# Layer 1's neighbour sums in a two-layer graph kernel: from four parts in two PSUM banks to five parts in four

## The chip, the cores and the metric

The kernel runs on one core of a Trainium2 chip. The metric is the device time of the whole kernel in microseconds (us). Five engines of the core work side by side, each through its own program in order: TensorE (PE: matmuls, and weight loads, PEld), VectorE (DVE), ScalarE (ACT), GpSimd (POOL) and SyncE (SP). They meet through semaphores.

## The reference

`x` is 4096 x 64; `adj` is a 4096 x 4096 matrix of zeros and ones with about 8 ones in a row. Two layers run one after the other, each with a residual:

```python
h = relu(layernorm(x))                      # layer 0
w = adj / max(adj.sum(1), 1e-8)
log_ij = logmap(h[i], h[j])                 # on the Poincare ball, c = 1
x = x + expmap(0, einsum('ij,ijc->ic', w, log_ij) @ W0 + b0)

h = relu(layernorm(x))                      # layer 1
support = h @ W1
rank = cumsum(adj != 0, axis=1); deg = rank[:, -1:]
k = minimum(deg, 100); pos = rank - (deg - k)
w = mask * where(pos > 0, 0.5 ** (k - pos), 0)
x = x + w @ support + b1
```

Layer 0 needs a vector for each pair of neighbours; layer 1 is a product of a sparse 4096 x 4096 weight matrix with `support`. A neighbour's weight in layer 1 is a power of two set by its rank in the row.

## The kernel before, in words

All of it is one function, `tile_gnn_kernel`. Nodes are kept in 32 blocks of 128 rows, in four quarters of eight blocks (`QB = 8`). First `adj` is streamed in and turned into fp8 masks, `masks[q]`, one per quarter of rows (`load`: SP's DMA at L873, transposes at L888, ACT's copy at L891), and each row's neighbours are searched and listed (L917, L981 and others). A row's first six listed neighbours are its "ell" part; the further ones of long rows are the "tail", kept in extra columns for a quarter's blocks.

**Layer 0** then runs in units 0 to 16. A unit: `gather` (L1139) issues one indirect DMA on POOL for each list column (12 for the ell part of two blocks, 9 or 6 for tails in units 5 to 16), which fetches the neighbours' rows into the tile `g`, of which there are two; so the gathers of unit n start only when unit n-2 has done with its `g`, whose last reader is DVE's L1234 (and L1198 in some units). `tail_rows` makes one-hot tiles on ACT (L1156, L1163), transposes them on PE (L1169), copies them (L1170) and selects the tail's own rows with PE matmuls (L1178). `differ` subtracts on DVE (L1192, L1208, L1211) and squares on ACT (L1222). `weigh` starts with L1234, the sum of squares, and goes back and forth between DVE and ACT to L1251. `total` scales the tails' one-hots on ACT (L1261), sums tails on PE (L1266) and the ell part on DVE (L1281, L1288); `total_tail` is L1295.

**Between the layers**, `middle(m, stage)` takes a group of blocks, `groups = [(0,8),(8,8),(16,8),(24,6),(30,2)]`: stage 0 (L1314 and on) finishes layer 0's sum; stage 1 (L1334, transposes L1302, matmuls L1345) multiplies by W0 into a tile of the pool `ps_w` named `words`; stage 2 is tanh, residual and layernorm on DVE and ACT (L1353 to L1359, helpers up to L739); stage 3 multiplies by W1 (L1386, L1390 into `ps_t`) and splits the result into three bf16 terms by ACT (L1403) and DVE (L1405), which go to `sup[c]`. The rows are shifted by one, so the last block of each half of the matrix comes with its group, but the last of the other groups' eight only with the next group: group 0 alone fills seven blocks.

`step` (L1412) turns the masks of a quarter into the layer's weights by adding exponents on DVE, 15 of them a quarter.

**Layer 1's sums** are `collect(c, p, n)` (L1414): part `c` of the sum's terms, quarter `p` of the rows, pair `n` of its blocks. `sums` lists the parts as (first block, blocks, groups that must be ready): 16, 7, 6 and 3 blocks. For each of two row blocks, `nb` matmuls of 128 x 128 masks with 128 x 192 of `sup[c]` (L1422; in the last part one more with the bias, L1430) add up in a PSUM tile of 2 x 256 fp32 a partition, from the pool `ps_a` with two buffers. `pool` decides how it leaves: false, by DVE (L1441 sums the three terms, L1445 adds it to `acc`); true, by ACT (L1436 copies it to `mr` or `dg`) and three additions on POOL (L1438). Each part has 16 collects of 2 x `nb` matmuls: 1024 at L1422 altogether, 24 evictions by DVE and 40 by ACT and POOL. The first part is DVE's, the second and third ACT's and POOL's, the fourth half and half. After the last one a flag is read back and the kernel ends.

**The order.** `at(when, fn)` collects the whole work in a plan with a due time; collects are due 20 after the latest of their groups and quarter. The plan is sorted, gives each call a priority, and the tile framework's scheduler orders every engine's program by these and by what is ready in its own model of time. So an engine's order is fixed when the program is built; a late operand makes an engine wait at that instruction. In the built program of before, only 14 of the sums stand on PE ahead of unit 13's L1169; the other 498 of part 0 are spread from there on between the matmuls of the later units.

Of the kernel before, what the change touches and what calls it, by code (L numbers as in the profile page):

```python
# [11 lines left out]
F32 = mybir.dt.float32  # L12
# [7 lines left out]
P = 128  # L20
# [528 lines left out]
def kernel(  # L549
# [66 lines left out]
    with ExitStack() as fast:  # L616
# [174 lines left out]
        late = masks[NQ - 1].bitcast(F32).rearrange("p b c -> p (b c)")  # L791
# [44 lines left out]
        ps_a = fast.enter_context(tc.tile_pool(name="ps_a", bufs=2, space=PSUM))  # L836
        ps_w = fast.enter_context(tc.tile_pool(name="ps_w", bufs=2, space=PSUM))
# [7 lines left out]

        groups = [(0, 8), (8, 8), (16, 8), (24, 6), (30, 2)]

        sums = [(0, 16, (0, 1)), (16, 7, (2,)), (23, 6, (3,)), (29, 3, (4,))]


        def bf(at, n):
# [3 lines left out]
        sup, o = [], 0  # L855
        for c, (_, nb, _) in enumerate(sums):
            n = nb + (c == len(sums) - 1)
# [555 lines left out]

        def collect(c, p, n):  # L1414

            pool = 0 < c < len(sums) - 1 or (c == len(sums) - 1 and n >= 2)
            b0, nb, _ = sums[c]
            end = c == len(sums) - 1
            o = ps_a.tile([P, 2, 2 * P], F32, name="a_ps")
            for k in range(2):  # L1420
                for j in range(nb):
                    nc.tensor.matmul(  # L1422
                        o[:, k, 0:W3],
                        lhsT=masks[p][:, b0 + j, bass.ts(2 * n + k, P)],
                        rhs=sup[c][:, j, :],
                        start=(j == 0),
                        stop=(j == nb - 1 and not end),
                    )
                if end:
                    nc.tensor.matmul(  # L1430
                        o[:, k, 0:W3], lhsT=last, rhs=sup[c][:, nb, :], start=False, stop=True
                    )
            ab = acc[:, p * QB + 2 * n : p * QB + 2 * n + 2, :]
            if pool:
                ev = (lst if n % 2 else blk).tile([P, 2, W3], F32, name="dg" if n % 2 else "mr")
                nc.scalar.activation(ev, o[:, :, 0:W3], AF.Copy, scale=2.0**-W8_SHIFT)  # L1436
                for k in range(3):
                    nc.gpsimd.tensor_tensor(ab, ab, ev[:, :, k * D : k * D + D], ALU.add)  # L1438
                return
            red = lst.tile([P, 2, D], F32, name="wsb")  # L1440
            nc.vector.tensor_reduce(  # L1441
                red, o[:, :, 0:W3].rearrange("p k (n c) -> p k c n", n=3), AX.X, ALU.add
            )
            a = ab.rearrange("p k c -> p (k c)")
            nc.vector.scalar_tensor_tensor(  # L1445
                a, red.rearrange("p k c -> p (k c)"), 2.0**-W8_SHIFT, a, ALU.mult, ALU.add
            )
# [93 lines left out]
        for when, c, p in pairs:  # L1541
            t = max(t, when + 20.0)
            left[p] -= 1
            for n in range(QB // 2):
                at(t, collect, c, p, n)
                t += max(1.0, 0.2 * sums[c][1])
                if left[p] == 0 and n % 2:
                    at(t, write, p, n // 2)
# [43 lines left out]
```

## Time and profile before

| | |
|---|---|
| time, median of 3 runs | 752.56 us (748.73 to 755.61) |
| the profiled execution: time, span | 754.09 us, 752.2 us |
| busy: PE, PEld | 400.0 us (53%), 344.2 us (46%) |
| busy: DVE, ACT, POOL | 403.2 us (54%), 345.6 us (46%), 350.5 us (47%) |
| mean granted PE clock | 0.668 of full speed |
| gathers L1139, ell and tail | 288 instructions, 291.8 us of POOL |
| sums L1422 | 1024 matmuls, 109.1 us of PE |
| read from HBM | 83.11 MB |

The span is what the hardware profiler recorded; the device time has 1.89 us more around it. A line of the page's groups gives line, engine, operation, tiles, count, then busy us and mean ns of one, then the engine's idle time just before such instructions and who ended most of it ("issue": the profile shows nothing that was waited for; "remote": a semaphore from outside what it shows). In the table by stretches, each row has a stretch of the span and its length, then busy us and count for PE, PEld, DVE, ACT and POOL, the granted PE clock, the share of the DMA engines and GB/s.

### The profile page before, as it was taken

To read this page: it belongs to the slowest core of one execution; us is meant where nothing else is said; L and a number is where in the kernel's file an instruction comes from. 1 tells how busy PE (TensorE), PEld (TensorE's weight loads), DVE (VectorE), ACT (ScalarE), POOL (GpSimd) and SP (SyncE) were. 2 spreads that over 40 slices of the span, in tenths; PEclk is the share of its full clock that TensorE was granted. 3 is DMA by queue.
4 is the path that set the end of the run, shared out by engine and by line. 5 is a ranking of instruction groups with operands and counts; after the bars stand their busy time and mean duration, and the time that the engine had idled before them with its cause. 6 is when DMAs were issued, how large, how long until landed. Compare 5 with 4: busy or idle time off the path is not lost.

```text
span 752.2 us, 11841 instructions
## 1 busy us (share of the span) xinstructions
PE 400.0 (53%) x4094; PEld 344.2 (46%) x4094; DVE 403.2 (54%) x1557; ACT 345.6 (46%) x791; POOL 350.5 (47%) x423
## 2 busy tenths in 40 slices
PE   3742465643632628636067351452274378979881
PEld 3542353532531517535054241342164168979871
DVE  7742386734880518927169463793623136764520
ACT  6742465733842529836156251343242214565430
POOL 1374606246475440562705454587274713007892
PEclk9865576755855757855556555555556669988997
DMA  8994567755963536956201111221111110000001
GB/s 310 384 323 137 192 217 245 261 168 154 343 198 94 180 95 217 322 164 191 33 17 17 29 34 23 44 38 26 30 27 33 28 15 13 14 10 1 2 22 40
DMA packets 42858, 88.23 MB, mean 117 GB/s; under 512 B 14756, under 2 KB 20388, under 8 KB 42660
## 3 DMA queue, kind: packets, MB, share of 16 engines
q1 hardware_dynamic: 21458, 72.93, 26.9%
q0 software_dynamic: 9504, 10.67, 8.1%
q10 hardware_dynamic: 11826, 3.78, 2.3%
q8 instruction: 34, 0.56, 0.3%
q14 instruction: 36, 0.29, 0.1%
HBM read 83.11 MB, written 4.24 MB: 116 GB/s over the span
## 4 chain that ended last, share of the span: by engine, by line
DVE 23%; another core or an unknown queue 22%; PE 20%; ACT 16%; issue 10%; DMA 5%; ACTq 2%; POOL 1%; DVEq 0%; SPq 0%; POOLq 0%
PE a_ps L1422 9%; ACT mask L891 7%; PE a_ps L888 3%; DVE mask L1412 3%; PE words L917 2%; DMA room<-in_adj 2%; DVE cand L981 1%; DVE tl L1095 1%; DVE tb L1093 1%; ACT oh L1156 1%; PE sel L1266 1%; POOL acc L1438 1%; DVE wsb L983 1%; DMA w_sb<-in_L_gnn_weight 1%
## 5 line engine op out<-in xcount | busy, mean ns | idle before, releaser
L1139 POOL DMA_INDIRECT g<-tab_d,ell_i x192 | 198.0, 1031 | 266.2 <-DVE d L1234 84.7
L891 ACT ACTIVATE mask<-a_ps 128x1024 fp8e5<-128x1024 bf16 x128 | 128.2, 1028 | 113.8 <-remote 84.6
L888 PE MATMUL a_ps<-ident_b,room 128*128 128x128 bf16 x1024 | 107.4, 272 | 63.6 <-ACT mask L891 37.4
L1422 PE MATMUL a_ps<-room,mask 128*128 128x192 bf16 x1024 | 109.1, 260 | 32.5 <-issue 25.9
L888 PEld LDWEIGHTS <-room 128*128 128x128 bf16 x1024 | 92.9, 158 | 69.9 <-issue 68.0
L1139 POOL DMA_INDIRECT g<-tab_d,tail_i x96 | 93.8, 977 | 50.8 <-issue 28.1
L1422 PEld LDWEIGHTS <-mask 128*128 128x128 fp8e5 x1024 | 93.1, 104 | 41.1 <-issue 39.3
L917 PEld LDWEIGHTS <-mask 128*128 128x128 fp8e5 x1024 | 49.5, 115 | 107.6 <-ACT mask L891 56.7
L917 PE MATMUL words<-pk,mask 128*128 128x64 bf16 x1024 | 61.1, 219 | 70.2 <-ACT mask L891 44.4
L981 DVE MAX8 cand<-wsb 128x8 f32<-128x256 f32 x96 | 40.5, 422 | 88.5 <-ACT wsb L928 80.8
L1266 PE MATMUL sel<-d,mr 128*128 128x65 f32 x192 | 41.3, 379 | 20.2 <-issue 16.7
L1266 PEld LDWEIGHTS sel<-d,mr 128*128 128x128 f32 x192 | 39.0, 295 | 24.9 <-issue 19.6
L1438 POOL TENSOR_TENSOR acc<-acc,dg 128x128 f32<-128x128 f32 x60 | 28.2, 469 | 36.0 <-ACT dg L1436 33.9
L1412 DVE TENSOR_TENSOR mask<-mask 128x1024 int16<-128x1024 int16 x60 | 40.7, 678 | 6.6 <-ACT q__5085 L1241 4.0
L1441 DVE TENSOR_REDUCE wsb<-a_ps 128x128 f32<-128x384 f32 x24 | 13.3, 555 | 46.0 <-remote 27.8
L1261 ACT ACTIVATE mr<-oh,r 128x128 f32<-128x128 bf16 x96 | 29.3, 389 | 18.0 <-DVE acc L1445 7.5
L1438 POOL TENSOR_TENSOR acc<-acc,mr 128x128 f32<-128x128 f32 x60 | 28.5, 475 | 14.6 <-ACT mr L1436 12.7
L1169 PE MATMUL mi<-ident_b,oh 128*128 128x128 bf16 x96 | 12.6, 283 | 38.1 <-ACT oh L1163 28.2
L904 PE MATMUL words<-gn,ones_b 1*128 1x352 bf16 x32 | 12.3, 390 | 35.1 <-ACT cn L931 20.9
L1156 ACT ACTIVATE oh<-row,tail_r 128x128 bf16<-128x128 bf16 x96 | 29.4, 389 | 3.2 <-DVE tail_r L1109 3.1
L1169 PEld LDWEIGHTS <-oh 128*128 128x128 bf16 x96 | 8.9, 128 | 41.1 <-ACT oh L1163 29.2
L1170 ACT COPY mr<-mi 128x768 bf16<-128x768 bf16 (+1 forms) x20 | 13.5, 674 | 30.6 <-PE mi L1169 12.2
(332 smaller groups left out, 775.1 us busy)
## 6 DMA issues: line engine op xcount, KB each, us to landing
room<-in_adj SPq DMA_DIRECT2D x128, 512.0 KB
g<-tab_d,ell_i POOLq DMA_INDIRECT x192
hp_d<-mask SPq DMA_DIRECT2D x1, 1560.0 KB
g<-tab_d,tail_i POOLq DMA_INDIRECT x96
mr<-hp_d ACTq DMA_DIRECT2D x8, 146.2 KB
tab_d<-mask POOLq DMA_DIRECT2D x2, 520.0 KB
hi<-tab_d ACTq DMA_DIRECT2D x16, 65.0 KB
mask<-in_x SPq DMA_DIRECT2D x2, 512.0 KB
```

What stands on the lines that cost most here:

```text
L888: nc.tensor.transpose(a_ps[:, k, :], upper[:, e : 2 * HC : 2 * JH], ident_b)
L891: nc.scalar.activation(masks[q][:, j0 : j0 + QB, bass.ts(b, P)], a_ps, AF.Copy, scale=2.0**-ONE, saturate=False,)
L917: nc.tensor.matmul(w, lhsT=masks[q][:, j, bass.ts(b, P)], rhs=pk, start=False, stop=True, skip_group_check=True,)
L981: nc.vector.max(out=top, in_=src)
L1139: nc.gpsimd.indirect_dma_start(out=g[:, k, :], out_offset=None, in_=tab_d, in_offset=bass.IndirectOffsetOnAxis(ap=i, axis=0),)
L1156: nc.scalar.activation(oh[:, k, :], row128, AF.Abs, bias=tail_r[:, t0 + k // TB, k % TB : k % TB + 1], scale=-1.0,)
L1169: nc.tensor.transpose(mp[:, k - k0, :], oh[:, k, :], ident_b)
L1261: nc.scalar.activation(mr[:, k, :], u["oh"][:, k, :], AF.Copy, scale=r[:, e2 + k : e2 + k + 1])
L1266: nc.tensor.matmul(ag[:, k // TB, :], lhsT=mr[:, k, :], rhs=d[:, e2 + k, :], start=(k % TB == 0), stop=(k % TB == TB - 1),)
L1412: nc.vector.tensor_tensor(m[:, :, j, :], m[:, :, j, :], m[:, :, j - 1 if j else JH - 1, :], ALU.add)
L1422: nc.tensor.matmul(o[:, k, 0:W3], lhsT=masks[p][:, b0 + j, bass.ts(2 * n + k, P)], rhs=sup[c][:, j, :], start=(j == 0), stop=(j == nb - 1 ...
L1438: nc.gpsimd.tensor_tensor(ab, ab, ev[:, :, k * D : k * D + D], ALU.add)
```

## The change

`sums` has five parts instead of four: the former first part of 16 blocks is cut into 7 blocks that need group 0 and 9 that need group 1. `collect` takes its PSUM tile from `ps_a` (`a_ps`) for even `n` and from `ps_w` (`words`) for odd `n`: four banks in turn instead of two, of which `middle` uses the two of `ps_w` as well. The flag `pool`, now named `late`, is shifted by one, so that both first parts go out by DVE, and the others as before.

```diff
-        sums = [(0, 16, (0, 1)), (16, 7, (2,)), (23, 6, (3,)), (29, 3, (4,))]
+        sums = [(0, 7, (0,)), (7, 9, (1,)), (16, 7, (2,)), (23, 6, (3,)), (29, 3, (4,))]
...
         def collect(c, p, n):
 
-            pool = 0 < c < len(sums) - 1 or (c == len(sums) - 1 and n >= 2)
+            late = 1 < c < len(sums) - 1 or (c == len(sums) - 1 and n >= 2)
             b0, nb, _ = sums[c]
             end = c == len(sums) - 1
-            o = ps_a.tile([P, 2, 2 * P], F32, name="a_ps")
+            pool, name = (ps_w, "words") if n % 2 else (ps_a, "a_ps")
+            o = pool.tile([P, 2, 2 * P], F32, name=name)
...
-            if pool:
+            if late:
```

Counts: 1024 sums at L1422 and 40 evictions by ACT and POOL stay; DVE's evictions go from 24 to 40. In the changed file, lines from L1419 on are one higher (L1422 is L1423, L1436 is L1437, L1441 is L1442). The built programs differ in order on PE from the 4,645th row on: 126 sums now stand ahead of unit 10's first L1266, 154 ahead of unit 11's L1169, and all 224 of part 0 ahead of unit 12's L1169 (before: 14, 14 and 14). Ahead of unit 16's L1266 stand 582 (before 554), after the last L1386 188 (before 247).

## The prediction

> **What bounds the kernel now.** I read the span and the shares of the chain first.
>
> ```profile
> span 752.2 us, 11841 instructions
> DVE 23%; another core or an unknown queue 22%; PE 20%; ACT 16%; issue 10%; DMA 5%; ACTq 2%; POOL 1%; DVEq 0%; SPq 0%; POOLq 0%
> ```
>
> No engine carries the chain. A third of it is time in which an engine waited for nothing visible (22% and 10%). Where, the groups and the timeline say: POOL's gathers of units 11 to 16 come in bursts, 436.7 to 463, 476.3 to 506.8 (A, unit 12), 507.1 to 529.6 (B, 13), 543.3 to 570.3 (C, 14), 579 to 605 (D, 15) and 626.8 to 634.1 (E, 16). Each waits for L1234 of the unit two before it:
>
> ```profile
> L1139 POOL DMA_INDIRECT g<-tab_d,ell_i x192 | 198.0, 1031 | 266.2 <-DVE d L1234 84.7
> L1422 PE MATMUL a_ps<-room,mask 128*128 128x192 bf16 x1024 | 109.1, 260 | 32.5 <-issue 25.9
> ```
>
> Next the table by stretches: busy us and counts of PE, PEld, DVE, ACT, POOL, then PE's clock.
>
> ```profile
> 476.30:502.60 26.30, 11.49 (x74) 9.20 (x72) 21.88 (x68) 10.96 (x28) 21.10 (x18) 0.50 0.23 45
> 513.50:532.00 18.50, 1.29 (x9) 0.83 (x8) 4.32 (x18) 4.00 (x11) 12.29 (x13) 0.50 0.20 33
> 579.00:584.50 5.50, 5.27 (x64) 5.13 (x63) 2.26 (x11) 1.06 (x4) 4.28 (x5) 1.00 0.13 24
> 584.50:607.00 22.50, 5.25 (x25) 2.46 (x25) 2.29 (x7) 4.59 (x15) 15.55 (x17) 0.57 0.19 27
> 634.10:664.10 30.00, 28.99 (x311) 27.59 (x310) 23.53 (x76) 19.91 (x60) 0.00 (x0) 0.94 0.04 10
> ```
>
> In burst D PE runs 64 matmuls in 5.5 us, then 25 in 22.5 us; the timeline shows how:
>
> ```profile
> 593.10 0.32 PE L1422 MATMUL a_ps<-room,mask 128*128 128x192 bf16 x1 [1.75 <-issue]
> 595.23 0.32 PE L1422 MATMUL a_ps<-room,mask 128*128 128x192 bf16 x1 [1.81 <-issue]
> 597.34 0.32 PE L1422 MATMUL a_ps<-room,mask 128*128 128x192 bf16 x1 [1.79 <-issue]
> ```
>
> One matmul in 2.1 us, with nothing to wait for. I call it the crawl. It lasts until 2 to 3 us after the burst (D ends at 605, PE recovers at 607; B 529.6 and 532; C 570.3 and 573), and DVE and ACT slow with it. It begins when PE has issued some 110 to 170 instructions, weight loads counted, since the burst began (fewer where the other engines issued much, as in B). Burst A alone shows none: PE had only 74 matmuls there in 26.3 us. What causes it no view shows. From A, unit 11's way to its L1234:
>
> ```profile
> 487.03 2.82 PE L1266 MATMUL sel<-d,mr 128*128 128x65 f32 x12 [5.16 <-issue]
> 494.44 1.20 PE L1178 MATMUL sel<-mr 128*128 128x65 bf16 x18
> 498.60 0.56 DVE L1208 TENSOR_TENSOR d<-g,sel 128x384 f32<-128x384 f32 x1
> 500.95 1.55 DVE L1234 TENSOR_REDUCE d<-g 128x21 f32<-128x1344 f32 x1
> 507.09 0.94 POOL L1139 DMA_INDIRECT g<-tab_d,ell_i  x1 [0.31 <-issue]
> ```
>
> B starts at 507.09 with no wait: the inputs were ready 3.8 us earlier (503.3). That slack is all.
>
> [...] PE holds at 3.51 us before L1266 at 674.6 while sums stand behind it. [...] near 718 PE waits 0.57 us for ACT's copy after each 24 sums. [...] the table has 0.50 in A and 1.00 at 579.
>
> **The change part by part**, against the span of 752.2. Time of the sums: 91 in 8.57 us at 575.7, 0.1 us each; at half clock 8 in 1.49, 0.19.
>
> (1) Early sums. Group 0's terms are complete at about 471.7, when the 14 sums of before start. In the changed order 126 sums stand ahead of unit 10's L1266 and 154 ahead of unit 11's L1169. By 482 to 486 some 75 to 115 are done, of which the ones since 476.3 with their loads make 110 to 170 PE instructions: I take the crawl to set in there, ahead of L1266. It lifts at 506.8 + 2.5 = 509.3, having let some ten through. Left are then 30 to 70 sums, 3 to 10 us at 0.1 to 0.15, partly beside DVE's arrears. From L1266's start to L1234's end took 502.5 - 487.0 = 15.5 us before. So L1234 ends at 509.3 + 15.5 + 3.8 = 528.6 (3.8: the low half of 3 to 10, as DVE is behind too), and B starts there: +21.5. Bounds: 0 without a crawl, +28 with all 70 sums in line.
>
> (2) DVE's 16 new evictions, 0.555 + 0.29 = 0.845 us by L1441 and L1445, 13.5 us in all. [...] the row says 555 and is used. In A DVE is busy 21.88 of 26.3, and eight evictions, 6.8 us, stand ahead of unit 11's L1234: 2.4 us over what is free. That lies under (1)'s wait while it crawls. Without that cover it costs 2.4 to 6.8 less the slack 3.8, 0 to 3.
>
> (3) Burst B carries 56 more sums ahead of unit 11's L1266 and unit 12's L1169, so it crawls with more left over; but L1334, which held PE 7.5 us in B's crawl, now stands behind them. Between -1 and +5: +1.5 to C. C and D keep their steps: their bursts have no more sums than before.
>
> (4) Unit 13's L1266 in D has 100 sums ahead since D's start instead of 124: 24 x 0.1, -2.
>
> (5) 626.8 to 664: PE is full (28.99 of 30.0) and now has some 150 sums less. The step is bound by unit 15's way through L1169, L1178 and ACT's L1261 to group 2's last L1403 at 663.7; sums in front cost it 3 to 4 us, but half of group 2's L1386 now stand behind unit 15's L1266: -2 (0 to -4).
>
> (6) The end, 664 to 739. POOL takes 2.71 us for two collects, 40 of them 54 us, over 72 us (first addition 666.7, last 739): there is a hole of 9.84 us before 678, when PE stands at L1266. PE is busy 62.5 of these 72. Four banks let sums stand ready for POOL across the holes, and 59 fewer sums come after the last L1386, 59 x 0.089 = 5.3 us. PE has 27 fewer in all. So PE's floor is 60, POOL's 57: gain up to 12, none if POOL is late by group 4. I take -7.5. ACT's 40 copies keep their count.
>
> (7) A wait that is new: `middle`'s tile `words` holds one of `ps_w`'s two banks from L1334 to L1356, so a sum with odd n may stop PE, with L1266 or L1169 behind it and DVE and POOL behind these. In A, L1334 stands after unit 11's L1178 (182 sums), so it isn't in (1). Later each case costs at most an eviction, 0.85 us; five groups, 0 to 4. I take 0, since `ps_a`'s two banks give PE 48 sums' or so of other work, 4 us.
>
> Gathers, DMAs, POOL's and SP's programs keep their counts and order; no queue gets more. Sum: 21.5 + 1.5 - 2 - 2 - 7.5 = +11.5, a span of 763.7; with 1.9 around it 765.6. The profiled execution lay 1.5 above the median of the runs (754.09 against 752.56), so 764.1.
>
> **Rivals.** *No crawl in A* (other side). If its onset needs what A lacks, the sums fall into PE's free 14.8 us of A (112 x 0.1 = 11.2), unit 11's L1178 is done by 502 and B keeps 507. Only the gains stay: -11.5, 741. For it: A never crawled, PE at full clock would be at L1266 at 487. Against: C and D both crawl with a burst like A's. It decides at whether L1178 ends before about 502.
>
> *No crawl, but queues.* At half clock, 126 sums take 22 us and L1266 comes at 495; with (2) B starts 2 to 8 us late, and B's 56 sums cost 0 to 3: +6 - 11.5, 747 (742 to 753). PE at 0.50 in A speaks for it[...].
>
> *The crawl costs twice.* What A leaves over meets B's crawl before unit 12's L1169: then its 15.5 us follow B's end, (3) is +10 to +20, and the time 778. B's crawl with so few instructions of PE (x9 in 18.5 us) speaks for it; that unit 12's work is short, against.
>
> *The end gains nothing*, POOL being the bound: within the range, 764 + 7.5 = 771.5, part of the forecast's own spread.
>
> **Chances.** Forecast 0.50 (own range 757 to 772), twice 0.12 (772 to 788), queues 0.22, no crawl 0.16 (736 to 746). About 1% is what a measurement of this kernel can tell: faster is under 745.0, slower over 760.1. Slower: 0.44 of the forecast and 0.12, 0.56. Faster: 0.15 and 0.08 of the queues, 0.23. Within: the rest, 0.21. The range 741 to 780 leaves out half of the last case and a third of the second.
>
> **What would show it.** Right: L1423 at 2.1 us steps between about 485 and 507; a hole of some 20 us on POOL before B, at 528; then C at 566, and the 9.84 us hole in POOL's additions gone. Wrong at (1): B at 507 to 510, PE dense through A at clock 1.00. Wrong at (3): C over 32 us behind 543. Wrong at (6): PE again waiting at unit 16's L1266, and over 70 us from group 2's last L1403 to POOL's last addition.

## The result

The changed kernel took 775.16 us (median of 4 runs, 772.13 to 779.82) against 752.69 us for the kernel before (4 runs): a ratio of 1.0308, with a 95% interval of 1.0236 to 1.0379. It is slower by 22.5 us where 11.5 was forecast. The profiled execution took 774.28 us, its span is 772.5.

Lines of the page of the changed kernel:

```profile
span 772.5 us, 11874 instructions
...
another core or an unknown queue 24%; PE 21%; DVE 17%; ACT 16%; issue 10%; DMA 5%; POOL 3%; ACTq 2%; DVEq 0%; SPq 0%; POOLq 0%
...
L1139 POOL DMA_INDIRECT g<-tab_d,ell_i x192 | 198.2, 1032 | 288.4 <-DVE d L1234 100.2
```

Busy times hardly moved. POOL's idle time ahead of the gathers did: 288.4 us instead of 266.2, so the gathers start later. The timeline of the changed kernel in burst A and after it:

```profile
494.03 0.32 PE L1423 MATMUL words<-room,mask 128*128 128x192 bf16 x1 [2.19 <-issue]
...
501.07 0.32 PE L1423 MATMUL words<-room,mask 128*128 128x192 bf16 x1 [1.79 <-issue]
502.48 1.61 PE L1423 MATMUL words<-room,mask 128*128 128x192 bf16 x9 [1.08 <-issue]
...
507.02 1.25 PE L1266 MATMUL sel<-d,mr 128*128 128x65 f32 x10
...
511.46 0.73 PE L1178 MATMUL sel<-mr 128*128 128x65 bf16 x18
...
492.65 0.56 DVE L1442 TENSOR_REDUCE wsb<-a_ps 128x128 f32<-128x384 f32 x1 [8.55 <-PE a_ps L1423]
...
519.18 1.55 DVE L1234 TENSOR_REDUCE d<-g 128x21 f32<-128x1344 f32 x1
...
520.99 1.23 POOL L1139 DMA_INDIRECT g<-tab_d,ell_i  x1 [21.99 <-DVE w L1198]
```

Sums one to three at a time, 0.7 to 3.5 us apart, with nothing to wait for: the crawl, now in burst A, from about 478 to 502.4. The new evictions carry it to DVE: L1442 waits 8.55 us for crawling sums, and what unit 10 still has to do on DVE stands behind it. Unit 10's first L1266 starts at 505.7 and most of them at 507, instead of at 487; unit 11's L1234 ends at 520.7 instead of 502.5, and POOL stands 22 us before B. The table by stretches has it as PE's count. Of the 84 matmuls in A's 26.3 us only 24 come in the last 20.7; then 137 come in the 21.9 us of POOL's pause.

```profile
472.80:499.10 26.30, 11.08 (x84) 7.41 (x81) 9.93 (x32) 5.26 (x18) 20.11 (x21) 0.66 0.22 40
478.40:499.10 20.70, 5.75 (x24) 2.55 (x23) 6.55 (x21) 3.85 (x14) 15.73 (x17) 0.57 0.17 27
499.10:521.00 21.90, 12.86 (x137) 11.20 (x136) 17.57 (x52) 5.75 (x12) 0.01 (x1) 0.86 0.06 14
```

To find the rest I took the starts of the bursts, and R, the start of group 2's last L1403, from two traces of each kernel (us; the second traces are e7 and e6 below):

| step | before | changed | difference | forecast |
|---|---|---|---|---|
| start to A | 476.3, 473.1 | 472.8, 472.8 | -1.9 | 0 |
| A to B | 30.8, 30.7 | 48.2, 49.4 | +18.1 | +21.5 |
| B to C | 36.3, 37.0 | 39.7, 36.9 | +1.7 | +1.5 |
| C to D | 35.6, 35.6 | 39.9, 39.9 | +4.3 | 0 |
| D to E | 47.8, 48.0 | 46.1, 46.9 | -1.4 | -2 |
| E to R | 36.9, 36.9 | 42.3, 42.3 | +5.4 | -2 |
| R to the end | 88.6, 87.4 | 83.5, 85.5 | -3.5 | -7.5 |
| span | 752.2, 748.7 | 772.5, 773.8 | +22.7 | +11.5 |

Three steps lie above the forecast: C to D by 4.3 us, E to R by 7.4 and the end by 4.0. A to B and the start lie 3.4 and 1.9 under it.

**C to D.** Timeline of the changed kernel, first ACT, then PE:

```profile
590.18 0.37 ACT L1403 CAST room<-t 128x256 bf16<-128x256 f32 x1 [17.31 <-remote]
591.07 0.69 PE L1386 MATMUL t<-w_sb,room 64*128 64x64 f32 x2 [13.99 <-DVE room L1405]
596.27 0.73 PE L1178 MATMUL sel<-mr 128*128 128x65 bf16 x10
```

ACT's cast comes only after C's crawl. Behind it PE still has five of group 1's pairs L1386 and L1390: four stand ahead of all of unit 13's L1178, the fifth ahead of its last ten. Before, all were done by 558.8, ahead of the crawl, and L1178 came at 574.3, just after it. Five pairs at 0.86 us are the 4.3.

Burst C of the changed kernel has no sums at all (all 224 of part 0 are done, and those of part 1 have not begun), and PE had issued nothing since 555.9. It stands all the same, with nothing to wait for:

```profile
567.42 1.12 PE L1266 MATMUL sel<-d,mr 128*128 128x65 f32 x4 [11.49 <-issue]
```

**E to R.** PE in the kernel before:

```profile
649.56 0.60 PE L1302 MATMUL o<-ident,y 128*64 128x128 f32 x4
```

PE in the changed kernel, ACT's last cast, and the stretch from E's end to R:

```profile
673.79 1.06 PE L1302 MATMUL o<-ident,y 128*64 128x128 f32 x4 [7.44 <-DVE y L711]
...
679.13 3.94 PE L1266 MATMUL sel<-d,mr 128*128 128x65 f32 x18
683.00 0.69 PE L1386 MATMUL t<-w_sb,room 64*128 64x64 f32 x2
...
689.05 0.41 ACT L1403 CAST room<-room 128x256 bf16<-128x256 f32 x1 [0.49 <-DVE room L1405]
...
654.00:689.10 35.10, 20.33 (x120) 17.90 (x120) 23.80 (x82) 21.40 (x64) 0.00 (x0) 0.57 0.04 10
```

Group 2's second half of L1386 stands behind unit 15's L1266. Its first L1302 of stage 3 waits 7.4 us for the end of stage 2 (L711) and comes 27.1 us after E's start (646.7); before, it came 22.8 us after E's start. PE has no sums here but four at 687 and runs at 0.57 of its clock (before, 0.94 from E's end to R).

**The end.** POOL's additions, in the kernel before and in the changed one:

```profile
666.70 1.52 POOL L1438 TENSOR_TENSOR acc<-acc,dg 128x128 f32<-128x128 f32 x3 [32.60 <-ACT dg L1436]
678.05 1.83 POOL L1438 TENSOR_TENSOR acc<-acc,mr 128x128 f32<-128x128 f32 x3 [9.84 <-ACT mr L1436]
```

```profile
698.05 1.52 POOL L1439 TENSOR_TENSOR acc<-acc,dg 128x128 f32<-128x128 f32 x3 [44.13 <-ACT dg L1437]
```

The hole of 9.84 us is gone, and the additions span 62.0 us instead of 72.3, from the first start to the last. But the first comes 9.0 us after R instead of 3.0, since only nine of part 2's sums stand on PE ahead of unit 16's L1178 and group 3's L1345, and a collect needs 14. So 10.3 us are gained and 6 given back.

### The profile page after: what moved, and what is told of

Same layout as the page of the kernel before. It is cut to its first block, busy times and chain, and to the rows that moved or that the text cites. A ratio compares the mean times of both kernels' runs of the same rounds, so it can differ in the third digit from the quotient of the medians.

```text
span 772.5 us, 11874 instructions
## 1 busy us (share of the span) xinstructions
PE 396.5 (51%) x4094; PEld 339.3 (44%) x4094; DVE 414.8 (54%) x1589; ACT 343.5 (44%) x791; POOL 348.6 (45%) x423
## 4 chain that ended last, share of the span: by engine, by line
another core or an unknown queue 24%; PE 21%; DVE 17%; ACT 16%; issue 10%; DMA 5%; POOL 3%; ACTq 2%; DVEq 0%; SPq 0%; POOLq 0%
ACT mask L891 6%; PE words L1423 4%; PE a_ps L1423 4%; PE a_ps L888 3%; POOL acc L1439 2%; DMA room<-in_adj 2%; PE words L917 2%; PE sel L1266 2%; DVE mask L1412 2%; ACT mr L1261 2%; DMA tab_d<-mask 1%; ACT oh L1156 1%; DVE cand L981 1%; PE t L1386 1%
## 5 line engine op out<-in xcount | busy, mean ns | idle before, releaser
L1139 POOL DMA_INDIRECT g<-tab_d,ell_i x192 | 198.2, 1032 | 288.4 <-DVE d L1234 100.2
L888 PE MATMUL a_ps<-ident_b,room 128*128 128x128 bf16 x1024 | 102.3, 263 | 57.4 <-ACT mask L891 38.5
L1423 PEld LDWEIGHTS <-mask 128*128 128x128 fp8e5 x1024 | 93.6, 105 | 61.5 <-issue 59.0
L888 PEld LDWEIGHTS <-room 128*128 128x128 bf16 x1024 | 89.1, 157 | 64.4 <-issue 63.7
L1139 POOL DMA_INDIRECT g<-tab_d,tail_i x96 | 92.3, 961 | 49.0 <-issue 27.7
L917 PE MATMUL words<-pk,mask 128*128 128x64 bf16 x1024 | 58.1, 214 | 71.7 <-ACT mask L891 54.0
L917 PEld LDWEIGHTS <-mask 128*128 128x128 fp8e5 x1024 | 46.3, 111 | 105.7 <-ACT mask L891 65.6
L1423 PE MATMUL words<-room,mask 128*128 128x192 bf16 x512 | 60.7, 261 | 39.7 <-issue 23.9
L1423 PE MATMUL a_ps<-room,mask 128*128 128x192 bf16 x512 | 59.1, 264 | 9.8 <-issue 6.3
L1266 PE MATMUL sel<-d,mr 128*128 128x65 f32 x192 | 39.2, 362 | 30.5 <-issue 17.9
L1266 PEld LDWEIGHTS sel<-d,mr 128*128 128x128 f32 x192 | 36.7, 276 | 32.0 <-issue 18.7
L1439 POOL TENSOR_TENSOR acc<-acc,dg 128x128 f32<-128x128 f32 x60 | 27.9, 465 | 48.2 <-ACT dg L1437 46.9
L1412 DVE TENSOR_TENSOR mask<-mask 128x1024 int16<-128x1024 int16 x60 | 40.5, 675 | 3.8 <-ACT mask L968 3.8
L904 PE MATMUL words<-gn,ones_b 1*128 1x352 bf16 x32 | 11.9, 379 | 39.9 <-ACT cn L931 20.9
L1442 DVE TENSOR_REDUCE wsb<-words 128x128 f32<-128x384 f32 x20 | 11.0, 552 | 36.4 <-remote 33.5
L1442 DVE TENSOR_REDUCE wsb<-a_ps 128x128 f32<-128x384 f32 x20 | 11.0, 552 | 36.0 <-remote 12.3
L1169 PE MATMUL mi<-ident_b,oh 128*128 128x128 bf16 x96 | 12.4, 284 | 33.6 <-ACT oh L1163 20.3
```

Source lines behind the costliest of these rows:

```text
L888: nc.tensor.transpose(a_ps[:, k, :], upper[:, e : 2 * HC : 2 * JH], ident_b)
L917: nc.tensor.matmul(w, lhsT=masks[q][:, j, bass.ts(b, P)], rhs=pk, start=False, stop=True, skip_group_check=True,)
L1139: nc.gpsimd.indirect_dma_start(out=g[:, k, :], out_offset=None, in_=tab_d, in_offset=bass.IndirectOffsetOnAxis(ap=i, axis=0),)
L1266: nc.tensor.matmul(ag[:, k // TB, :], lhsT=mr[:, k, :], rhs=d[:, e2 + k, :], start=(k % TB == 0), stop=(k % TB == TB - 1),)
L1412: nc.vector.tensor_tensor(m[:, :, j, :], m[:, :, j, :], m[:, :, j - 1 if j else JH - 1, :], ALU.add)
L1423: nc.tensor.matmul(o[:, k, 0:W3], lhsT=masks[p][:, b0 + j, bass.ts(2 * n + k, P)], rhs=sup[c][:, j, :], start=(j == 0), stop=(j == nb - 1 ...
```

## The experiments

The theory to be tested: part 0's early sums set off a crawl in burst A. Its rivals: DVE's 16 evictions in line, the shared banks, PE's half clock. The runs fell on different chips. On three of them (13, 14 and 0) the kernel before takes 753 to 765 us and crawls, as in the result; on two (7 and 9) it takes 566 to 567, and no trace from them shows PE in single steps through a burst. Ratios are always to the kernel before on the same chip; A, B, E and R as above.

**e7, e6, e19: the two kernels again.** No edit.

> The kernel before, for a trace on this chip. Where the time is near 566 us, PE's single matmuls at 2.1 us steps with nothing to wait for are missing in all bursts, and the gathers of units 10 to 15 follow each other with pauses under 3 us (753 us: pauses of 13 to 22 us after A's predecessor, B, C and D). Where it is near 752, they are there.

> The changed kernel itself once more, beside the kernel before on the same chip. If this chip runs the kernel before near 566 us, with burst after burst of gathers on POOL and no crawl, the crawl theory says that the change's 17 us between A's and B's start can't appear: A to B stays at POOL's 30 to 31 us and the ratio is 0.99 to 1.01. If the cost is queues (sums and evictions ahead of unit 11's L1208), it appears without a crawl too: A to B 35 or more and the ratio 1.01 to 1.03. If the chip runs the kernel before near 752, A to B is 45 to 50 again and the ratio 1.02 to 1.04.

> The changed kernel. On a chip without the crawl: A to B is 30 to 31 us, bound by POOL's own gathers, and of the change's costs only the order after E's start is left (step to group 2's last L1403 23 to 25 us where four parts had 17.4), against a gain of the end: ratio 0.998 to 1.008. On a chip with the crawl: ratio 1.023 to 1.034 as before, A to B 47 to 50.

Chip 13: e7 750.50 us with the same steps; e6 775.29 us, ratio 1.0281 (1.0230 to 1.0332), A to B 49.4. Chip 0: e19 784.63 against 764.6, ratio 1.0283 (1.0212 to 1.0353), A to B 49.0, E to R 43.0. The cost and its places repeat. What the whole change costs on a chip without the crawl was not measured; the nearest is e13 below, 0.9979 on chip 9.

**e1, e12: five parts in two banks.**

```diff
-            pool, name = (ps_w, "words") if n % 2 else (ps_a, "a_ps")
+            pool, name = ps_a, "a_ps"
```

> Five parts as in the change, but all sums in ps_a's two banks (half of the change). 84 sums stand ahead of unit 10's L1266 (126 in the change, 14 before), 112 ahead of unit 11's L1169 (154 and 14). Crawl theory: PE still issues over 55 sums with their loads in burst A before L1266, so the crawl sets in there and A's start to B's start is 42 to 50 us (before 30.8, changed 48.2). Theory of queues alone (no crawl, only sums and evictions in line): the two banks let PE go no faster than DVE's evictions, and A to B is 34 to 40. Theory that the shared banks make group 2 late: E's start to group 2's last L1403 comes back from 42.8 to about 37 to 38; theory of the cold PE: it stays at 41 to 44 where PE's clock there is under 0.7. The end keeps two banks, so from group 2's L1403 to the span's end about 88 as before. Time: about 772 by the crawl, 760 by queues.

> Five parts in two banks again. On a chip like the one of the result: 84 sums ahead of unit 10's L1266, but no more than 28 of them ahead of DVE's evictions. By the crawl theory with an onset at 110 to 170 instructions of PE in a burst it crawls in A, A to B 40 to 50. If the pace matters, not the count (72 sums at a slower pace showed none), A to B is 31 to 38. E's start to group 2's last L1403 36 to 38, since the order has 99 sums there. Ratio 1.010 to 1.025 by the count, 0.998 to 1.008 by the pace.

e1 fell on chip 7: 570.07 against 566.38, ratio 1.0032 (1.0001 to 1.0062). There is no crawl there whose cost its time could show, but its trace answers another question. Burst A:

```profile
346.00:376.70 30.70, 19.04 (x180) 16.74 (x179) 28.41 (x87) 10.91 (x28) 24.56 (x21) 0.83 0.23 42
```

180 matmuls of PE and 87 instructions of DVE under one burst, and B starts 31.0 us after A. Without the crawl all the early sums and their evictions fit under POOL. e12, the same kernel on chip 13, has 87 matmuls and 33 instructions of DVE in the same 30.7 us: 775.48 against 754.3, 1.0260 (1.0205 to 1.0314), A to B 47.5. So the fifth part alone brings the cost. First DVE, then PE:

```profile
505.48 0.56 DVE L1442 TENSOR_REDUCE wsb<-a_ps 128x128 f32<-128x384 f32 x1 [11.44 <-remote]
506.09 2.40 PE L1423 MATMUL a_ps<-room,mask 128*128 128x192 bf16 x14 [12.88 <-issue]
```

Here PE doesn't go in single steps. It runs its sums densely up to 493.2; the fourth collect's are done at 489.4. DVE is free from 494.0 and takes them at 505.5, and PE goes on in the bank that this frees. What DVE waits for is not shown. So the loss in A can come as single steps on PE or as one standstill.

E to R is 38.6 and C to D 34.8 there. With the four banks but without the fifth part (e11 below) they are 31.1 and 35.5. So those two losses need both halves of the change.

**e2, e11: four parts in four banks.** `sums` and the flag as before the change, the banks as after it.

> Four parts as before, with four banks in turn (the other half of the change). 21 sums stand ahead of unit 10's L1266. Crawl theory: none in burst A, A to B within 2 us of 30.8. E's start to group 2's last L1403: if the shared banks make it late, over 40; if the lack of sums does (cold PE), about 36 to 38, since the sums are there again. The end: 83 as in the changed kernel instead of 88. Time 745 to 749 by crawl and cold PE, 750 to 755 by the shared banks.

> Four parts in four banks again. On a chip like the one of the result: 21 sums ahead of unit 10's L1266, so no crawl in A by the crawl theory, A to B 30 to 33; E's start to group 2's last L1403 36 to 38, with the sums there; from there to the span's end 84 to 88. Ratio to before 0.990 to 1.000. If four banks by themselves cost what the change costs, the ratio is over 1.02.

e11, chip 13: 755.92, ratio 0.9997 (0.9970 to 1.0024), A to B 30.8, C to D 35.5, E to R 31.1, from R to the end 92.3. Banks alone cost and bring nothing there: from E to the end 123.5 us against 125.5 and 124.3. e2, chip 7: 563.74, ratio 0.9916 (0.9886 to 0.9946), 0.8% faster there.

**e8: cut at block 3. e3: cut at block 11, so that part 0 needs group 1.** Five parts and four banks; stage 3 finds its part by block.

```diff
-        sums = [(0, 7, (0,)), (7, 9, (1,)), (16, 7, (2,)), (23, 6, (3,)), (29, 3, (4,))]
+        sums = [(0, 3, (0,)), (3, 13, (0, 1)), (16, 7, (2,)), (23, 6, (3,)), (29, 3, (4,))]    # e8
+        sums = [(0, 11, (0, 1)), (11, 5, (1,)), (16, 7, (2,)), (23, 6, (3,)), (29, 3, (4,))]   # e3
```

> Five parts and four banks, cut at block 3 instead of 7: 72 sums instead of 126 stand ahead of unit 10's L1266, 78 instead of 154 ahead of unit 11's L1169, with the same 16 early evictions by DVE. On a chip with the crawl: it sets in late or not at all in A, A to B 31 to 42 (changed 48.2). On a chip without it: A to B 30 to 32, and the ratio 0.99 to 1.00, since the end has the four banks and 176 sums after the last L1386.

> Five parts and four banks, with 40 evictions by DVE as in the change, but cut at block 11 instead of 7, so that the first part needs group 1 and can't run in burst A; 21 sums stand ahead of unit 10's L1266, 28 ahead of unit 12's gathers' use. Crawl theory: A to B within 2 us of 30.8. If it were the number of parts or DVE's 16 more evictions by themselves, A to B stays over 40. E's start to group 2's last L1403 36 to 39 (130 sums stand between unit 14's L1178 and that point). Time 744 to 752 by the crawl; 770 and over if the evictions are the cause.

e8, chip 13: 752.07, ratio 0.9988 (0.9952 to 1.0024), A to B 30.4. Burst A:

```profile
471.90:502.40 30.50, 18.70 (x120) 13.90 (x118) 28.01 (x88) 10.92 (x28) 23.78 (x22) 0.60 0.23 43
```

No crawl in A, with 72 sums ahead of unit 10's L1266 instead of 126, and with nine of DVE's early evictions within the burst (e18 below has eight, e12 and the changed kernel fewer). That is for the early sums as the cause, and against the evictions by themselves. But PE issued 238 instructions here (120 and 118), loads counted: a count of 110 to 170 since the burst's start is not what sets the crawl off. B to C lost 7.5 us here (44.1). e3 fell on chip 7: 563.06, ratio 0.9940 (0.9908 to 0.9971), A to B 30.9; there it tells nothing on the crawl, and shows that five parts with 40 evictions by DVE need not cost.

**e10: the kernel before plus 112 sums that nobody reads,** placed like the early sums.

```diff
+        def extra(tiles, m):
+            for p in range(tiles):
+                o = ps_a.tile([P, 2, 2 * P], F32, name="a_ps")
+                for k in range(m):
+                    nc.tensor.matmul(o[:, 0, 0:W3], lhsT=masks[p % 2][:, k % 7, bass.ts(p // 2, P)],
+                        rhs=sup[0][:, k % 7, :], start=True, stop=True)
...
+        at(ready[0] + 20.0, extra, 8, 14)
```

> The kernel before plus 112 matmuls of the sums' shape (128 x 192, with weight loads) at the place where the change has its early sums, ahead of unit 10's L1266, into ps_a's banks; nobody reads them and DVE evicts nothing of them. On a chip like the one of the result: crawl theory says that PE's instructions alone set it off: PE in single steps of 2.1 us from about 478 to 2 to 3 us after A's end, A to B 45 to 52 us (before 30.8). Theory of DVE's evictions or of the waits between PE and DVE: no crawl, A to B under 37, PE dense. On a chip without the crawl A to B stays 30 to 34 by either.

Chip 13: 763.46, ratio 1.0120 (1.0071 to 1.0168); A to B 41.4, between the two expectations. First PE, then DVE:

```profile
487.60 4.64 PE L1454 MATMUL a_ps<-room,mask 128*128 128x192 bf16 x28 [7.64 <-remote]
502.88 0.29 DVE L1295 TENSOR_TENSOR y<-y,sel 128x130 f32<-128x130 f32 x1 [15.36 <-remote]
```

PE stops after 70 of the sums for 7.6 us on a semaphore that comes from outside what the profile shows, and DVE stands 15.4 us. PE's instructions alone bring 10.6 us of the 18, as standstills and not as single steps.

**e5, e15, e18: one matmul of seven in part 0.** The terms of blocks 0 to 5 are left out of the sums; all evictions stay.

```diff
-                for j in range(nb):
+                for j in range(nb) if c else range(nb - 1, nb):
```

> The changed kernel with one matmul of the seven in each chain of part 0 (the terms of blocks 0 to 5 are left out of the sums; 192 of 1056 matmuls less). All 16 early evictions of DVE stay in burst A, with 20 matmuls instead of 126 ahead of unit 10's L1266. Crawl theory: no crawl in A, A to B 30 to 34. Theory of DVE's evictions: A to B 36 or more. C and D then have no more in front than before: B to C 35 to 37, C to D 35 to 37. E's start to group 2's last L1403: only 49 sums stand between unit 14's L1178 and the end of that step; by the cold PE it stays over 41, with PE's clock under 0.7 there.

> The changed kernel with one matmul of seven in each chain of part 0 (the terms of blocks 0 to 5 left out) once more. On a chip like the one of the result: all 16 of DVE's early evictions, 20 sums instead of 126 ahead of unit 10's L1266. If PE's instructions set off the crawl in A, there is none and A to B is 30.5 to 34; if DVE's evictions or their waits do, A to B is over 38. E's start to group 2's last L1403 40 to 43, as the order there is like the changed kernel's and no sums are left.

> The changed kernel with one matmul of seven in each chain of part 0 (the terms of blocks 0 to 5 left out). On a chip with the crawl: all of DVE's 16 early evictions with 20 sums ahead of unit 10's L1266 instead of 126. If PE's instructions set off the crawl in A, A to B is 30.5 to 34; if the evictions do, over 38. On a chip without it: ratio 0.997 to 1.003 as twice before.

Chips 7 and 9: ratios 1.0001 (0.9970 to 1.0032) and 0.9992 (0.9963 to 1.0021), A to B 29.5 and 29.6. Chip 0: 757.81 against 764.6, 0.9889 (0.9808 to 0.9970); A to B 36.9, again between the expectations. PE, then ACT and DVE:

```profile
486.65 0.48 PE L1423 MATMUL a_ps<-room,mask 128*128 128x192 bf16 x2 [4.80 <-DVE wsb L1442]
506.07 0.48 PE L1169 MATMUL mi<-ident_b,oh 128*128 128x128 bf16 x3 [3.90 <-issue]
505.22 0.80 ACT L1170 COPY mr<-mi 128x768 bf16<-128x768 bf16 x1 [4.25 <-remote]
509.69 0.56 DVE L1208 TENSOR_TENSOR d<-g,sel 128x384 f32<-128x384 f32 x1 [2.52 <-remote]
```

There are no single steps. The first sums wait for DVE's evictions, which stand between `step`'s L1412 and the tail search, and unit 10's L1266 starts 16.4 us after A's start instead of 10.7. From 501 on, PE, ACT and DVE wait again for nothing that is shown. L1208 comes 30.7 us after A's start (22.3 before), and from L1266's start to L1234's end it takes 20.2 us instead of 15.5. So not all of the 6 us are queues. An estimate: 5.7 us at L1266 less the slack of 3.8 leave some 2 us for them, and the other 4 belong to those waits. In e8's order of DVE's work the queues cost nothing. The 10.6 us of e10 and these 6 come near the 18.1, but both hold such waits, and the kernel before was not traced on chip 0: the sum is not shown.

**e9: 84 matmuls in the gap after unit 15's L1178.**

```diff
+            if n == 15:
+                at(z + 1.0, warm, u, 6, 14)     # matmuls of u["mt"] into a_ps, read by nobody
```

> The changed kernel plus 84 matmuls of 128 columns, whose result nobody reads, on PE between unit 15's L1178 and the L1302 of group 2, where PE stands idle for 7.4 us in the changed kernel. On a chip like the one of the result (before near 752): if the step from E's start to group 2's last L1403 (42.4 us changed, 37.1 before) is longer because PE, without sums to do, runs its chain at half clock, the clock there rises from 0.57 to over 0.75, the eight L1386 and L1390 behind unit 15's L1266 take about 2 us instead of 3.6, and the step is 38 to 40, the time 2 to 4 us under the changed kernel's. If it is the order alone (half of group 2's L1386 behind unit 15's L1266), the step stays at 42 or grows by what the 84 matmuls last.

Chip 13: 778.58, ratio 1.0334 (1.0275 to 1.0394). E to R is 41.6, but the clock is at 0.56 around the L1386, no higher than in the changed kernel, so this run doesn't decide between order and clock.

```profile
671.00:686.10 15.10, 14.22 (x66) 12.21 (x66) 7.42 (x24) 9.91 (x29) 0.00 (x0) 0.56 0.03 8
```

**e13, e16: group 2 takes its bank earlier.** e13 moved all of group 2's `middle` up in the plan, and so left unit 13's last additions out of its sums (L1327 runs 22.9 us ahead of that unit's L1295); e16 moves only the taking of `words` and its first matmul.

```diff
+                if m == 2 and k == 0:
+                    at(max(z, TLOADED + 4.0 + 12.0 * m) + z0 - 10.0 - 8.0, begin, m)   # e16: takes words, L1334
```

> The changed kernel with group 2's `middle` due 8 us earlier in the plan. In the built order its L1334 and first L1345 then stand ahead of unit 14's L1178 instead of behind 48 sums after it, and all eight of its second L1386 and L1390 ahead of unit 15's L1266 instead of behind it. Part 0 stands as in the changed kernel, and all 512 sums of parts 0 and 1 are again done before unit 14's L1266, so PE has no sums in the step. On a chip like the one of the result: if the order made the step from E's start to group 2's last L1403 longer, it falls from 42.4 us to 35 to 38 with the clock still near 0.57, and the time by 4 to 7 us, to 768 to 771; if the half clock did, it stays over 41. A to B stays 47 to 50.

> The changed kernel, with group 2's tile `words` taken and its first matmul (L1334 in the changed kernel) called 8 us earlier in the plan; nothing else moves in the plan. In the built order this alone puts that matmul 110 sums earlier, ahead of unit 14's L1169, the first four L1345 into unit 14's L1178, and all eight of group 2's L1386 ahead of unit 15's L1266 instead of half behind it. All 512 sums of parts 0 and 1 are still done before unit 14's L1266. On a chip with the crawl: by the order, E's start to group 2's last L1403 falls from 42.4 us to 35 to 38, with PE's clock there still under 0.7, and the time to 768 to 771 (ratio 1.018 to 1.024); by the half clock it stays over 41 and the ratio at 1.028. On a chip without the crawl: the step is 17 to 20 us by the order (it was 23 to 25 where group 2's L1386 stood behind, and 17.4 with four parts).

e13 fell on chip 9 (567.53, ratio 0.9979, 0.9938 to 1.0020; E to R 26.7) and doesn't tell. e16, chip 14: 771.13 against 754.86, ratio 1.0220 (1.0172 to 1.0267), A to B 49.1, E to R 37.9. Views of PE:

```profile
664.49 1.06 PE L1302 MATMUL o<-ident,y 128*64 128x128 f32 x4 [0.17 <-DVE y L711]
...
674.48 0.63 PE L1397 MATMUL t<-w1n_b,room 64*128 64x64 f32 x2
...
678.14 3.99 PE L1266 MATMUL sel<-d,mr 128*128 128x65 f32 x18
```

```profile
649.60:680.60 31.00, 23.83 (x131) 20.25 (x131) 19.23 (x59) 20.08 (x59) 0.00 (x0) 0.51 0.04 9
```

L1302 no longer waits, L1386 and L1390 (here L1393 and L1397) are done ahead of unit 15's L1266, and 4.5 of the 5.4 us are back, at a clock of 0.51. So the order made the loss, not the half clock; and the order hangs on the place at which the bank is taken. The gain is read from the step: the ratio's interval meets that of e6.

**e14, e17: part 0 held back to unit 14.** Four parts, four banks.

```diff
+        def hold(u):
+            s = sup[0][:, 0, 0:W3]
+            nc.vector.scalar_tensor_tensor(
+                s, u["d"][:, u["e2"], 0:1].to_broadcast([P, W3]), 0.0, s, ALU.mult, ALU.add)
```

> Four parts in four banks, with all sums of part 0 held back until unit 14's differences are there: one DVE instruction adds 0 times a column of unit 14's `d` to the first terms of `sup[0]`, and the sums wait for it. No sum runs in bursts A to D. On a chip like the one of the result: burst D's crawl (584 to 607 before) then has neither unit 13's L1266 nor unit 14's L1169 and L1178 behind 124 sums; if these ran before the crawl, D's start to E's start falls from 47.9 us to 30 to 40, and the time by up to 10 us, as PE then has some 120 us of work after E's start: 742 to 750. If D crawls as long with what is left, D to E is 44 to 48 and the time over 755, since all sums come later. On a chip without the crawl: slower than before by 1 to 4%.

> Four parts in four banks with part 0's sums held back to unit 14's differences, once more (on a chip without the crawl it took 1.015 of the time before). On a chip with the crawl: D's start to E's start 30 to 40 us instead of 47.9 if what stood behind the 124 sums now runs before D's crawl, time 742 to 750; 44 to 48 and over 755 if D crawls as long.

e17, chip 14: 749.10 against 754.86, ratio 0.9896 (0.9831 to 0.9960), D to E 33.7 instead of 47.9:

```profile
594.79 1.20 PE L1178 MATMUL sel<-mr 128*128 128x65 bf16 x18
617.43 0.95 POOL L1139 DMA_INDIRECT g<-tab_d,tail_i  x1 [6.93 <-DVE u L1235]
```

Unit 14's L1178 now runs 11 us into D instead of 41 us after its start. On this chip, where bursts crawl, it is 1.0% faster than the kernel before. e14 on chip 9: 576.20 against 566.99, 1.0149 (1.0076 to 1.0222): where they don't, it is slower.

## Why the prediction was wrong

The sign and the main mechanism held, the size did not: 22.5 us instead of 11.5. What failed is the pricing of the shared banks, (5) and (7), then the step C to D, put at nothing, and half of the gain at the end, (6). The total came within a factor of two partly by luck, as A to B and the start came out 5.3 us under the forecast.

**(1) early sums, +21.5: right in mechanism.** The crawl came where it was said, and B started 22.0 us after A's end, where the steps 2.5 + 15.5 + 3.8 make 21.8. It came out at +18.1 because A itself took 26.2 us instead of 30.5; DVE was busy 9.93 us in it instead of 21.88, and no gather took the 1.3 to 2.2 us that several took before. In the twenty traces A lasts 28.6 to 30.7 us where DVE is busy 21 to 29 us in it, and 26.2 to 28.0 where it is busy 7 to 11. But no run changes DVE's work alone, so that it draws the gathers out is likely and not shown. The onset by a count of instructions, on which (1) leaned, fell with e8 and with the changed kernel's own burst C. What sets the crawl off stays open: e8's 72 sums in twelve collects didn't, e12's 84 in six and e10's 112 in one run brought standstills, burst C stands without any sum, and some chips show none of it. On the queue that the trace names `instruction` the changed kernel has one packet of 16 KB in A, at 480.9, which took 1.1 us, so its transfer is not the delay; the kernel before has one in its A too, without a crawl. No run tries more.

**(2) evictions, nothing under the crawl, 0 to 3 without: not refuted.** e18 has 6 us without single steps, of which some 2 are queues by the estimate above; e5 and e15, the same kernel, cost nothing on chips 7 and 9.

**(3) B to C, +1.5 (measured +1.7), and (4) D to E, -2 (measured -1.4): right** in size. The two changed traces differ by 2.9 us in B to C, so the first may be luck.

**"C and D keep their steps: their bursts have no more sums than before": wrong, +4.3.** I counted sums and not the order of the rest. Five pairs of group 1's matmuls ran behind C's crawl and ahead of unit 13's L1178. This is read from the traces, and from e11 and e12, which don't have it; no run moves these pairs alone.

**(5) -2, with (7) taken as 0: the worst miss, +5.4.** (7) priced the shared banks as a wait of 0.85 us an eviction. What they did was to change the order when the program was built: group 2's L1334 takes its bank in turn with the sums and went behind 48 more of them, its second four L1345 behind another 26, and stages 2 and 3 came late. I saw half of L1386 behind unit 15's L1266 and let it take back no more than the 3 to 4 us that the sums in front had cost. The gain in unit 15's chain was there (its L1234 starts 22.6 us after E instead of 26.0), but the 10.9 us from that to R became 19.7. In e16 the place of the bank alone gives 4.5 us back.

**(6) -7.5: half of it, -3.5.** The holes closed for 10.3 us as forecast, but I let POOL start as soon after R as before; it started 6 us later, behind other groups' work in PE's order. In neither e11 (four parts) nor e16 (group 2's order mended) was more to be had: E to the end is 123.5 and 123.9 us, about 1 us under before (125.5 and 124.3).

**Rivals.** "No crawl in A" is what chips 7 and 9 do. "No crawl, but queues" is a part of e18 at most; its 126 sums at 0.19 us would take 24 us, not 22, which fits its own L1266 at 495. "The crawl costs twice" fell (B to C +1.7), though its time, 778, lay nearer than the forecast's.

**What stood in front, and the half clock.** In A ACT's L1163 waits 8.61 us for unit 10's L1266, which ends behind 140 sums: there the sums in front do hold up another engine. From E's end to R, with four sums in 35.1 us, PE's clock is 0.57. In the last stretch PE is busy 15.13 of 15.8 us, and the clock is 0.50:

```profile
673.80:689.60 15.80, 15.13 (x67) 12.75 (x68) 7.21 (x23) 9.69 (x29) 0.00 (x0) 0.50 0.02 6
```

So being busy with such work (mostly fp32 matmuls of 64 and 65 columns) did not lift it here. And the half clock was not what set the step: in e16 4.5 of the 5.4 us are back at a clock of 0.51.

## What to carry to other kernels

Work that fills an idle engine can stand ahead of what that engine owes to the others (here 126 sums ahead of unit 10's L1266, which came at 505.7 instead of 487); ask what the pause in it protected, and what happens when the engine slows, as PE did in burst A to one to three sums every 0.7 to 3.5 us. Buffers that two stages share can change the order in which a scheduler issues them, not only their waits: compare the built orders for every stage, not only for the part that was edited. Read a gain at the end from the first instruction of the bounding engine, not only from its holes.

## What was not expected of the hardware

The same kernel took 566 to 567 us on two chips and 753 to 765 us on three others. The gathers don't make the difference: the 192 ell ones take 1.02 to 1.04 us each on the slow kind and 1.07 to 1.08 on the fast one. Nor does the engines' busy time: in the same kernel PE is busy 407.5 us on the slow kind (e12) and 391.7 on the fast one (e1), with 87 and 180 matmuls in the 30.7 us after A's start. On the slow kind the waits are for nothing that the profile shows: in all 13 traces from it, "another core or an unknown queue" has 18 to 28% of the chain that ended last, and in none of the seven others does it appear. Of the 207 us between e12 and e1, 137 lie ahead of A, a stretch that no experiment here covers. Whether the kind belongs to the chip or to what else ran beside it, no run shows.

One must know which kind a measurement comes from before reading it: early sums cost 2.6% on the one (e12) and 0.3% on the other (e1).
